# Two attention layers on one core: the second layer's attention in one piece, the first layer's steps between projections, position pieces further apart

## The chip, the core and the metric

The kernel runs on one core of one Trainium2 chip. The metric is device time in microseconds (us), as the median of several runs; lower is better. Everything is fp32 (one operand pair is fp32r), and eight images go through two attention layers.

## What is computed

Two residual layers, each `x + attention(group_norm(x))`, over 8 images of 32 x 32 positions and 512 channels. The first layer has 16 heads of 32 channels and a projection; the second has 4 heads of 128 channels and adds logits of relative position, one for rows and one for columns. Cut from the reference:

```python
def _L0_conv_ref(x, w_qkv, w_proj, b_proj):
    qkv = xt @ w_qkv                                 # q, k, v: 16 heads of 32
    attn = jax.nn.softmax(jnp.einsum('bhid,bhjd->bhij', q * SCALE, k), axis=-1)
    out = jnp.einsum('bhij,bhjd->bhid', attn, v)
    return out @ w_proj + b_proj
def _L1_conv_ref(x, Wq, Wk, Wv, Wo, pos_emb_w, pos_emb_h):
    q = x @ Wq * scale; k = x @ Wk; v = x @ Wv       # 4 heads of 128
    scores = attn_q @ k + relative_logits(pos_q, pos_emb_w, pos_emb_h)
    return (jax.nn.softmax(scores, axis=-1) @ v) @ Wo
x = x + _L0_conv_ref(_gn(x), ...)
x = x + _L1_conv_ref(_gn(x), ...)
```

`_gn` is a group norm with 32 groups. Scores of one head are 1024 x 1024.

## The kernel before

An image is held channel-major (four tiles of 128 channels x 1024 positions). Its work is cut into stages, each a Python generator that records some instructions and then yields a number, the cost of what it recorded, in units of one group of four matmuls with 32 output columns:

- `load`: reads the image, transposes it on VectorE (DVE), takes statistics, norms it.
- `before_0`: q, k and v of the first layer, three matrix products. A product has 8 parts (`project_T`, `project_rows`); each part is 16 matmuls with 32 columns (`by_columns`, L206), one copy out of PSUM on ScalarE (ACT, L128), and a yield of 4.
- `attention_0`: 64 steps. A step is `front`, four matmuls of 32 rows into a four-bank tile `ps` (L278) and an exp of 128 x 2048 on ACT (L286), and then `back` of the step before: four matmuls of 32 columns into `acc` (L297) and an add to the running sum `es` on DVE (L306 the first time, L308 after). After every eight steps `finish` sums over partitions with four more matmuls (`su`, L317), takes a reciprocal and a check on DVE (L264, L245), and multiplies on GpSimd (L266).
- `after_0`, `norm_1`: the first layer's projection, added to the image on DVE (L482), and the second norm.
- `second`: q, k and v of the second layer. `position_logits` makes the position terms from q in four pieces. A piece is 64 small matmuls into a bank `pp` (L351, L358), then eight pairs of a cast on ACT (L373, into `posT`) and a subtraction on DVE (L374), both of which read `pp`. In the kernel before the pieces stand among the eight parts of the k product, after the second, fourth, sixth and eighth (`woven(keys, ..., 1, 2)`), and the v product follows.
- `attention_1`: 64 steps with full 128 x 128 matmuls: q times k (L387) and the position term (L388) into one bank, an exp of 128 x 512 on ACT (L390), e times v into `acc` (L399), a running sum on DVE (L408, L410), and every eight steps `su` (L418) with the same reciprocal, check and multiply.
- `after_1`: the second projection, added on DVE (L514), transposed (L516) and written out.

In what follows R stands for the four matmuls of L278, C for the four of L297, P for a part of a product, u for `su` of the first layer, x for the matmuls of a position piece, and F for the full-array matmuls of `attention_1`.

The stages of three images are recorded together. In round b, `side_by_side` walks through `attention_0` of image b and between its steps records from a chain of the other stages: `after_0`, `norm_1` and `second` of image b-1, with `after_1` of image b-2, then `attention_1` of image b-1 with the `load` of image b+1 woven into it, then `before_0` of image b+1. The total cost of that chain, divided by 65, is what is recorded after each attention step: rest is taken until `done` has caught up. In rounds 2 to 6 that is 408 units, 6.3 per step, of which `attention_1` is 144. A stage that yields 0 is taken whole at once, since nothing is counted as done. Rounds 0 and 8 have no partner on one side: in round 8, `attention_1` of the last image runs alone.

Tiles come from pools: three PSUM banks with the tag `bank` serve `pa`, `pp`, `su` and all of `attention_1`'s `ps` and `acc`; `ps` of the first layer is a single four-bank tile, so each R waits for the exp of the step before; `e0` has two buffers, so an exp waits for the add that last read the buffer it writes. The framework that records the instructions may move one ahead of others on its engine[...].

Of the kernel before, what the change touches and what calls it, by code (L numbers as in the profile page):

```python
# [9 lines left out]
F32 = mybir.dt.float32  # L10
# [7 lines left out]
P = 128  # L18
# [10 lines left out]
def quick_path(  # L29
# [100 lines left out]
    def load_weight(w, col0, name):  # L130
        t = mem.tile([P, CC, NB], F32, tag="w", name=name, bufs=2)
        nc.sync.dma_start(t, w.rearrange("(cc p) n -> p cc n", p=P)[:, :, col0 : col0 + NB])
        return t
# [76 lines left out]
    def project_T(xn, w, dsts, name):  # L210

        for m in range(CC):
            for h in range(NH):
                pa = bank(f"pa_{name}_{m}_{h}")
                for cc in range(CC):
                    by_columns(
                        pa,
                        w[:, cc, m * P : (m + 1) * P],
                        xn[cc][:, h * NB : (h + 1) * NB],
                        start=(cc == 0),  # L220
                        stop=(cc == CC - 1),
                    )
                evacuate(dsts(m)[:, h * NB : (h + 1) * NB], pa)
                yield CC

    def project_rows(xn, w, y, name):

        for t in range(NT):
            pa = bank(f"pa_{name}_{t}")
            for cc in range(CC):  # L230
                by_columns(
                    pa,
                    xn[cc][:, t * P : (t + 1) * P],
                    w[:, cc, :],
                    start=(cc == 0),
                    stop=(cc == CC - 1),
                )
            evacuate(y[:, t, :], pa)
            yield CC
# [100 lines left out]
    def position_logits(q, posT, b):  # L340

        qv = q.rearrange("p (i e) (x y) -> p e i x y", e=2, y=IW)
        G = NB // (IW * H1 // 2)
        for t in range(IW // G):
            pp = bank(f"pp_{b}_{t}", [P, G, H1 // 2, 32])
            for g in range(G):
                s = t * G + g
                for e in range(2):  # L350
                    nc.tensor.matmul(  # L351
                        pp[64 * e : 64 * e + 32, g],
                        pw_sb[:, IW - 1 - s : 2 * IW - 1 - s],
                        qv[:, e, :, :, s],
                        start=True,
                        stop=True,
                    )
                    nc.tensor.matmul(  # L358
                        pp[64 * e + 32 : 64 * e + 64, g],
                        ph_sb[:, IH - 1 - s : 2 * IH - 1 - s],  # L360
                        qv[:, e, :, s, :],
                        start=True,
                        stop=True,
                    )
            for h in range(H1):
                e, i = h % 2, h // 2
                by_y = posT[h].rearrange("p (x y) -> p y x", y=IW)
                by_x = posT[h].rearrange("p (x y) -> p x y", y=IW)
                for u, view in enumerate((by_y, by_x)):
                    view = view[:, t * G : (t + 1) * G]  # L370
                    rows = slice(64 * e + 32 * u, 64 * e + 32 * u + 32)
                    rests = slice(64 * (1 - e) + 32 * u, 64 * (1 - e) + 32 * u + 32)
                    nc.scalar.copy(view[rows], pp[rows, :, i])  # L373
                    nc.vector.tensor_sub(view[rests], pp[rows, :, i], view[rows].bitcast(F32))  # L374
            yield 2

    def attention_1(q, k, v, posT, b):

        steps = [(h, c, j) for h in range(H1) for c in range(NH) for j in range(NT)]
        state = {}  # L380

        def front(h, c, j):
            name = f"1_{b}_{h}_{c}_{j}"
            ps = bank(f"ps_{name}")
            keys = slice(j * P, (j + 1) * P)
            queries = slice(c * NB, (c + 1) * NB)
            nc.tensor.matmul(ps, k[h][:, keys], q[:, h, queries], start=True, stop=False)  # L387
            nc.tensor.matmul(ps, sel[:, keys], posT[h][:, queries], start=False, stop=True)  # L388
            e = mem.tile([P, NB], F32, tag="e1", name=f"e_{name}", bufs=3)
            nc.scalar.activation(e, ps, AF.Exp, scale=1.0 / math.sqrt(D1))  # L390
            return e

        def back(h, c, j, e):
            name = f"1_{b}_{h}_{c}_{j}"
            if j == 0:
                state["acc"] = bank(f"acc_{name}")
                state["first"] = e
            acc = state["acc"]
            nc.tensor.matmul(  # L399
                acc,  # L400
                v[:, j, h * D1 : (h + 1) * D1],
                e,
                start=(j == 0),
                stop=(j == NT - 1),
            )
            if j == 1:
                state["esum"] = mem.tile([P, NB], F32, tag="es1", name=f"es_{name}", bufs=2)
                nc.vector.tensor_add(state["esum"], state["first"], e)  # L408
            elif j > 1:
                nc.vector.tensor_add(state["esum"], state["esum"], e)  # L410
            if j < NT - 1:
                return
            state["ended"] = (h, c, hold(acc, name), state["esum"])

        def finish(h, c, held, esum):
            name = f"1_{b}_{h}_{c}"
            su = bank(f"su_{name}")
            nc.tensor.matmul(su, ones, esum, start=True, stop=True)  # L418
            normalise(q[:, h, c * NB : (c + 1) * NB], held, su, name)

        pending = None
        for at in steps:
            e = front(*at)
            ended = state.pop("ended", None)
            if pending is not None:
                back(*pending)
            pending = (*at, e)
            if ended is not None:
                finish(*ended)
            yield 2.25  # L430
        back(*pending)
        yield 1
        finish(*state.pop("ended"))

    def load(b, st):
# [56 lines left out]
    def second(b, st):  # L492

        xn = st.pop("xn")
        q = st["ao"] = mem.tile([P, H1, N], F32, tag="block", name=f"q1_{b}", bufs=BLOCKS)
        yield from project_T(xn, load_weight(Wq, 0, f"wq1_{b}"), lambda m: q[:, m, :], f"q1_{b}")
        posT = [chunk(f"posT_{b}_{h}", dtype=F32R) for h in range(H1)]
        k = [chunk(f"k1_{b}_{m}") for m in range(CC)]
        keys = project_T(xn, load_weight(Wk, 0, f"wk1_{b}"), k.__getitem__, f"k1_{b}")
        yield from woven(keys, position_logits(q, posT, b), 1, 2)  # L500
        v = mem.tile([P, NT, C], F32, tag="block", name=f"v1_{b}", bufs=BLOCKS)
        yield from project_rows(xn, load_weight(Wv, 0, f"wv1_{b}"), v, f"v1_{b}")
        st["at"] = (q, k, v, posT, b)

    def after_1(b, st):

# [18 lines left out]
    def woven(main, side, start, gap):  # L525

        for at, cost in enumerate(main):
            if at >= start and (at - start) % gap == 0:
                cost += next(side, 0)
            yield cost  # L530
        yield from side
# [27 lines left out]


    PRODUCT = 8 * CC
    SECOND = 3 * PRODUCT + 8 + 2.25 * H1 * NH * NT

    states = [{} for _ in range(B)]
    run(load(0, states[0]))
# [1 line left out]
    for b in range(B + 1):  # L567
        rest, total = [], 0
        s = [None] * 2 + states + [None] * 2
        past, last, here, coming = s[b : b + 4]  # L570
        incoming = load(b + 1, coming) if coming is not None else iter(())
        if last is not None:
            rest.append(after_0(b - 1, last))
            norm = norm_1(b - 1, last)
            if past is not None:
                rest.append(woven(after_1(b - 2, past), norm, 1, 1))
                total += PRODUCT
            else:
                rest.append(woven(iter(()), norm, 0, 1))
            rest.append(second(b - 1, last))  # L580
            rest.append(woven(later(lambda st: attention_1(*st.pop("at")), last), incoming, 4, 6))
            total += PRODUCT + SECOND
        else:
            rest.append(incoming)
        if coming is not None:
            rest.append(before_0(b + 1, coming))
            total += 3 * PRODUCT
        if here is not None:
            side_by_side(attention_0(here["q"], here["k"], here["v"], b), chain(*rest), total)
        else:  # L590
            run(chain(*rest))
# [493 lines left out]
```

## Time and profile before

| | |
|---|---|
| median of 3 runs | 4242.93 us (4241.28 to 4242.94) |
| the profiled execution | 4241.89 us |
| its span, first to last instruction | 4239.9 us |
| mean granted TensorE clock | 0.993 |
| busy: DVE, ACT, GpSimd | 2314.6, 1673.7, 248.7 us |
| L278 R, L297 C, 4096 matmuls each | 610.1, 553.3 us busy |
| L286 exp of the first layer, 512 | 1879 ns each |
| L308 running sum of the first layer, 384 | 2316 ns each |
| L264 reciprocal, 128 | 3355 ns each |
| L373 cast, L374 subtraction of the position pieces, 256 each | 480, 511 ns each |

Busy times are unions of an engine's intervals. The end of a matmul is modelled, so the distance from the start of one group to the start of the next is the better measure of what TensorE (PE) spends on it, and that is what is used below. A stage can be cut out by its times: in round 3, for instance, the k and v products with the position pieces last from about 1502 to 1596 us, the second layer's attention from 1596 to 1791 us, and the products for the next image from there to 1906 us. The last image's attention, alone, is at 4065 to 4198 us.

### The profile page before, as it was taken

To read this page: it belongs to the slowest core of one execution; us is meant where nothing else is said; L and a number is where in the kernel's file an instruction comes from. 1 tells how busy PE (TensorE), PEld (TensorE's weight loads), DVE (VectorE), ACT (ScalarE), POOL (GpSimd) and SP (SyncE) were. 2 spreads that over 40 slices of the span, in tenths; PEclk is the share of its full clock that TensorE was granted. 3 is DMA by queue.
4 is the path that set the end of the run, shared out by engine and by line. 5 is a ranking of instruction groups with operands and counts; after the bars stand their busy time and mean duration, and the time that the engine had idled before them with its cause. 6 is when DMAs were issued, how large, how long until landed. Compare 5 with 4: busy or idle time off the path is not lost.

```text
span 4239.9 us, 66880 instructions
## 1 busy us (share of the span) xinstructions
PE 4111.0 (97%) x29890; PEld 1367.7 (32%) x29890; DVE 2314.6 (55%) x2105; ACT 1673.7 (39%) x1793; POOL 248.7 (6%) x155
## 2 busy tenths in 40 slices
PE   7999999999999999999999999999999999999998
PEld 2222333223332233322333223332233322333343
DVE  2566566354763547635576355663556635467334
ACT  1553444324443244432444324443344333444131
POOL 0000000000000000100000000000000000000000
PEclk9999999999999999999999999999999999999999
DMA  4101110131101311012110121102210022000301
GB/s 120 36 21 46 31 40 1 36 95 31 40 1 41 90 31 40 1 56 75 37 34 1 72 61 44 26 1 75 65 51 1 1 81 65 22 35 1 86 16 21
DMA packets 320904, 172.23 MB, mean 41 GB/s; under 512 B 271424, under 2 KB 271456, under 8 KB 320608
## 3 DMA queue, kind: packets, MB, share of 16 engines
q1 hardware_dynamic: 320512, 167.81, 13.9%
q8 instruction: 236, 3.87, 0.4%
q14 instruction: 60, 0.49, 0.0%
q0 software_dynamic: 96, 0.07, 0.0%
HBM read 117.51 MB, written 50.33 MB: 40 GB/s over the span
## 4 chain that ended last, share of the span: by engine, by line
PE 85%; DVE 8%; ACT 4%; issue 1%; DMA 0%; POOL 0%; SPq 0%; DVEq 0%; ACTq 0%; POOLq 0%
PE ps L278 11%; PE pa_q L206 10%; PE ps L387 10%; PE pp L206 10%; PE acc L297 10%; PE acc L399 10%; PE pa_v L206 10%; PE pa_k L206 7%; ACT e L286 3%; PE ps L388 3%; DVE rc L264 2%; DVE posT L374 2%; DVE es L308 2%; ACT posT L373 2%; PE su L317 1%
## 5 line engine op out<-in xcount | busy, mean ns | idle before, releaser
L308 DVE TENSOR_TENSOR es<-es,e 128x2048 f32<-128x2048 f32 x384 | 889.2, 2316 | 893.8 <-ACT e L286 893.5
L286 ACT ACTIVATE e<-ps 128x2048 f32<-128x2048 f32 x512 | 962.1, 1879 | 818.1 <-PE ps L278 702.4
L278 PE MATMUL ps<-q,k 32*128 32x512 f32 x4096 | 610.1, 645 | 58.4 <-ACT e L286 58.2
L264 DVE RECIPROCAL rc<-su 128x512 f32<-128x512 f32 x128 | 429.2, 3355 | 306.1 <-PE su L317 287.3
L387 PE MATMUL ps<-q,k 128*128 128x512 f32 x1024 | 548.3, 617 | 14.2 <-DVE checks L245 13.6
L297 PE MATMUL acc<-e,v 128*32 128x512 f32 x4096 | 553.3, 611 | 1.0 <-ACT e L286 1.0
L390 ACT ACTIVATE e<-ps 128x512 f32<-128x512 f32 x512 | 305.3, 598 | 563.9 <-PE ps L388 460.4
L399 PE MATMUL acc<-e,v 128*128 128x512 f32 x1024 | 525.7, 596 | 0.7 <-ACT e L390 0.7
L266 POOL TENSOR_TENSOR q<-hd,rc 128x512 f32<-128x512 f32 x128 | 226.6, 1770 | 3467.1 <-DVE rc L264 3265.2
L388 PE MATMUL ps<-posT,sel 128*128 128x512 f32 x512 | 406.9, 795 | 0.0
L410 DVE TENSOR_TENSOR es<-es,e 128x512 f32<-128x512 f32 x384 | 277.0, 721 | 163.2 <-ACT e L390 152.5
L278 PEld LDWEIGHTS ps<-q,k 32*128 32x128 f32 x4096 | 166.1, 183 | 455.0 <-issue 202.3
L387 PEld LDWEIGHTS ps<-q,k 128*128 128x128 f32 x1024 | 174.3, 189 | 339.7 <-issue 261.5
L128 ACT COPY q<-pa_q 128x512 f32<-128x512 f32 x128 | 75.0, 586 | 427.2 <-PE pa_q L206 427.2
L206 PE MATMUL pa_q<-x0T,wq 128*32 128x512 f32 x2048 | 237.0, 600 | 5.4 <-DMA wq<-in_L_conv_w_qkv 4.7
L399 PEld LDWEIGHTS acc<-e,v 128*128 128x128 f32 x1024 | 193.0, 190 | 151.2 <-issue 110.4
L374 DVE TENSOR_TENSOR posT<-pp,posT 32x256 fp32r<-32x256 f32 x256 | 130.9, 511 | 195.0 <-ACT posT L373 193.1
L206 PE MATMUL pa_v<-wv,x1T 128*32 128x512 f32 x2048 | 230.5, 598 | 2.9 <-DVE posT L374 2.9
L206 PE MATMUL pa_k<-x1T,wk 128*32 128x512 f32 x2048 | 231.9, 595 | 0.6
L206 PE MATMUL pa_k<-x0T,wk 128*32 128x512 f32 x2048 | 232.3, 592 | 0.0
L206 PE MATMUL pa_v<-wv,x0T 128*32 128x512 f32 x2048 | 231.6, 592 | 0.0
L206 PE MATMUL pa_q<-x1T,wq 128*32 128x512 f32 x2048 | 228.3, 595 | 3.1 <-DVE x1T L192 3.1
(67 smaller groups left out, 2614.9 us busy)
## 6 DMA issues: line engine op xcount, KB each, us to landing
xs<-in_x SPq DMA_DIRECT2D x128, 128.0 KB, 3.2
d<-x0T SPq DMA_DIRECT2D x32, 512.0 KB, 3.6
x1T<-d SPq DMA_DIRECT2D x32, 512.0 KB, 5.9
d<-x1T SPq DMA_DIRECT2D x32, 512.0 KB, 2.6
x2T<-d SPq DMA_DIRECT2D x32, 512.0 KB, 6.3
out<-ot SPq DMA_DIRECT2D x256, 64.0 KB, 1.9
wq<-in_L_conv_w_qkv SPq DMA_DIRECT2D x8, 1024.0 KB, 7.7
wk<-in_L_conv_w_qkv SPq DMA_DIRECT2D x8, 1024.0 KB, 5.8
```

What stands on the lines that cost most here:

```text
L206: nc.tensor.matmul(out[columns, :], weights[:, columns], moving, start=start, stop=stop)
L264: nc.vector.reciprocal(rec, su)
L266: nc.gpsimd.tensor_tensor(dst, held, rec, op=ALU.mult)
L278: nc.tensor.matmul(ps[:, r, :], k[m][rows, j * P : (j + 1) * P], q[m][rows, h * NB : (h + 1) * NB], start=True, stop=True,)
L286: nc.scalar.activation(e, ps, AF.Exp, scale=D0 ** -0.5)
L297: nc.tensor.matmul(acc[r * D0 : (r + 1) * D0, :], v[:, j, c0 : c0 + D0], e[:, r, :], start=(j == 0), stop=(j == NT - 1),)
L308: nc.vector.tensor_add(state["esum"], state["esum"], e)
L387: nc.tensor.matmul(ps, k[h][:, keys], q[:, h, queries], start=True, stop=False)
L388: nc.tensor.matmul(ps, sel[:, keys], posT[h][:, queries], start=False, stop=True)
L390: nc.scalar.activation(e, ps, AF.Exp, scale=1.0 / math.sqrt(D1))
L399: nc.tensor.matmul(acc, v[:, j, h * D1 : (h + 1) * D1], e, start=(j == 0), stop=(j == NT - 1),)
L410: nc.vector.tensor_add(state["esum"], state["esum"], e)
```

## The change

Every step of `attention_1` now yields 0, so the whole of it is recorded between two steps of `attention_0`; `SECOND` loses its share, and the remaining rest, 264 units in rounds 2 to 6, is spread over the same 65 slots, 4.1 per step. The position pieces are woven into the k and v products together, after parts 2, 6, 10 and 14 of 16 instead of 2, 4, 6 and 8 of 8. In round 1, where the second norm has no other stage beside it, each of its two yields counts 12 units.

```diff
@@ attention_1
             if ended is not None:
                 finish(*ended)
-            yield 2.25
+            yield 0
         back(*pending)
-        yield 1
+        yield 0
         finish(*state.pop("ended"))
@@ second
         k = [chunk(f"k1_{b}_{m}") for m in range(CC)]
-        keys = project_T(xn, load_weight(Wk, 0, f"wk1_{b}"), k.__getitem__, f"k1_{b}")
-        yield from woven(keys, position_logits(q, posT, b), 1, 2)
-        v = mem.tile([P, NT, C], F32, tag="block", name=f"v1_{b}", bufs=BLOCKS)
-        yield from project_rows(xn, load_weight(Wv, 0, f"wv1_{b}"), v, f"v1_{b}")
-        st["at"] = (q, k, v, posT, b)
+        st["at"] = at = [q, k, None, posT, b]
+
+        def keys_and_values():
+            yield from project_T(xn, load_weight(Wk, 0, f"wk1_{b}"), k.__getitem__, f"k1_{b}")
+            at[2] = mem.tile([P, NT, C], F32, tag="block", name=f"v1_{b}", bufs=BLOCKS)
+            yield from project_rows(xn, load_weight(Wv, 0, f"wv1_{b}"), at[2], f"v1_{b}")
+
+        yield from woven(keys_and_values(), position_logits(q, posT, b), 1, 4)
@@ rounds
     PRODUCT = 8 * CC
-    SECOND = 3 * PRODUCT + 8 + 2.25 * H1 * NH * NT
+    SECOND = 3 * PRODUCT + 8
+
+    ALONE = 12
...
             else:
-                rest.append(woven(iter(()), norm, 0, 1))
+                rest.append(cost + ALONE for cost in norm)
+                total += 2 * ALONE
```

## The prediction, made before the changed kernel ran

> **What bounds the kernel now.** I read the page first, then the stages by windows, then the order of starts on PE, then ACT's and DVE's timelines at the position pieces.
>
> ```profile
> PE 4111.0 (97%) x29890; PEld 1367.7 (32%) x29890; DVE 2314.6 (55%) x2105; ACT 1673.7 (39%) x1793; POOL 248.7 (6%) x155
> PE 85%; DVE 8%; ACT 4%; issue 1%; DMA 0%; POOL 0%; SPq 0%; DVEq 0%; ACTq 0%; POOLq 0%
> ...
> 1502.00:1596.00 94.00, 88.28 (x961) 30.08 (x954) 50.44 (x53) 45.69 (x62) 6.45 (x2) 1.00 0.12 34
> 1596.00:1791.00 195.00, 191.51 (x740) 73.75 (x742) 133.59 (x127) 87.43 (x99) 15.04 (x11) 1.00 0.09 22
> ...
> 4066.00:4197.00 131.00, 131.00 (x332) 61.50 (x331) 68.12 (x77) 42.34 (x71) 10.70 (x7) 1.00 0.00 1
> ```
>
> PE is the bound; what can move is its idle time and what it loses between unlike groups. The windows are, in round 3, k and v with the position pieces, then the second layer's attention mixed with first-layer steps, and the last image's attention alone, where PE never stops. DMA is idle enough to leave aside.
>
> ```profile
> 1600.15 1.02 PE L399 MATMUL acc<-e,v 128*128 128x512 f32 x2
> 1601.01 1.02 PE L387 MATMUL ps<-q,k 128*128 128x512 f32 x2
> ...
> 1602.10 1.02 PE L399 MATMUL acc<-e,v 128*128 128x512 f32 x2
> ...
> 1604.04 1.02 PE L399 MATMUL acc<-e,v 128*128 128x512 f32 x2
> 1604.99 1.14 PE L278 MATMUL ps<-q,k 32*128 32x512 f32 x8
> 1606.07 1.07 PE L297 MATMUL acc<-e,v 128*32 128x512 f32 x8
> 1607.06 1.12 PE L387 MATMUL ps<-q,k 128*128 128x512 f32 x2
> ...
> 1608.26 1.02 PE L399 MATMUL acc<-e,v 128*128 128x512 f32 x2
> ...
> 1833.35 1.06 PE L297 MATMUL acc<-e,v 128*32 128x512 f32 x8
> 1834.23 3.62 PE L206 MATMUL pa_k<-x0T,wk 128*32 128x512 f32 x32
> 1837.78 1.14 PE L278 MATMUL ps<-q,k 32*128 32x512 f32 x8
> ```
>
> Read the starts. Within `attention_1` an L399 pair takes 0.86 ahead of L387 (1600.15 to 1601.01) and 0.95 ahead of R (1604.04 to 1604.99); L387 with L388 takes 1.09 after L399 (1601.01 to 1602.10) and 1.20 after C (1607.06 to 1608.26); C takes 0.99 ahead of L387 and 0.88 ahead of P; P takes 3.55 ahead of R and 3.43 ahead of its like. R takes 1.07. So the step costs 1.07 + 0.88 everywhere, plus 0.09 + 0.11 + 0.11 = 0.31 inside F and 0.11 inside P.
>
> ```profile
> 1510.52 1.14 PE L278 MATMUL ps<-q,k 32*128 32x512 f32 x8
> ...
> 1515.35 1.90 ACT L286 ACTIVATE e<-ps 128x2048 f32<-128x2048 f32 x1
> 1517.31 1.14 PE L278 MATMUL ps<-q,k 32*128 32x512 f32 x8 [1.22 <-ACT e L286]
> ...
> 1558.43 1.89 ACT L286 ACTIVATE e<-ps 128x2048 f32<-128x2048 f32 x1
> ...
> 1560.36 2.29 DVE L308 TENSOR_TENSOR es<-es,e 128x2048 f32<-128x2048 f32 x1 [1.12 <-ACT e L286]
> 1562.68 0.42 DVE L374 TENSOR_TENSOR posT<-pp,posT 32x256 fp32r<-32x256 f32 x1
> 1564.83 1.88 ACT L286 ACTIVATE e<-ps 128x2048 f32<-128x2048 f32 x1
> ...
> ACT posT L373 <- DVE posT L374: 20.3, 22, 2.5
> ```
>
> This is the wait that decides the case. A piece's casts and subtractions alternate: a cast, its subtraction, the next cast, some 2.1 us for two pairs. The exp of the R behind the piece stands after the fifth cast and ends 6.75 us after R's start; the next R starts at 6.79. And the second exp ends 6.4 us after the first (1560.32 to 1566.71), because the sixth subtraction stands behind the running sum that needs the first exp, and the seventh cast waits for it.
>
> [...] in an open stretch an exp starts 1.20 us after its R (1832.28 to 1833.48); the one above started 4.83 us after it, behind casts. [...]
>
> **The change, part by part.** The built program's queues show that it does what it says: in rounds 1 to 7 the 64 steps of `attention_1` stand in one run, with only one R split over it.
>
> *1. Mode changes.* Before, some 165 of the 512 first-layer steps stand inside F (143 R directly after an L399 pair, 20 after L418); after, 7. Each saves 0.31 - 0.11 = 0.20: 160 x 0.20 = 32; with other small shifts of order, -31.
>
> *2. `attention_1`.* In round 3: 64 steps x (1.09 + 0.86) = 124.8, 8 L418 pairs at 0.86 = 6.9, 23.5 R and C with their changes at 2.26 = 53.1, three u at 0.9 = 2.7, sum 187.5; it took 195. So 7.5 of stalls and split groups per round (5.6 to 7.8 in rounds 1 to 6, 3.3 in round 7, drops of the clock taken off: 47 in all). Alone it lost 1.4. After, each of rounds 1 to 6 has this 1.4, and an R split as 1, 2 and 1 matmuls, where one alone takes a whole slot (1.05 instead of 0.27): 2.1, and 0.3 for the norm's two small matmuls. 6 x 3.8 + 1.4 = 24, so -23, and -3 for the half R that stands at the start of the next stage now. The `load` moves with it: its transposes and statistics stay ahead of the run on DVE, its DMAs on SP keep their order against the weights, and nothing on PE needs them for 100 us, so they cost nothing; were that cover gone, four transposes and statistics are about 11 us per round. DVE is busy 68 of 131 us in such a run, by the last window, and GpSimd's multiply (1770 ns) comes every 16 us.
>
> *3. Position pieces, and denser steps around them.* This is the loss. The steps are now nearer to each other (4.1 units of rest instead of 6.3): between two R there is C and one P, 1.07 + 0.88 + 3.55 = 5.50 us, as at 1832.28 to 1837.78. Each piece holds up two exps, so two R wait, and as C and P stand behind R on PE, the whole wait counts. From the order of the queues in rounds 2 to 6, with R after the piece at 0:
> - piece 1: R, C, u, a quarter group of P, and already the next R: 1.07 + 0.88 + 0.86 + 0.33 = 3.14, against 6.78: 3.64. Behind that the second exp overwrites the first buffer of the running sum; the add that frees it stands behind the casts, a reciprocal (3.36) and its check (0.77), and ends at 13.3; exp to 15.2, R ready at 13.2: 2.0.
> - piece 2: room 5.50: 1.28. A transpose (1.24) stands in the chain: second exp to 13.7, room 6.78 + 5.50 = 12.28: 1.45.
> - piece 3: the reciprocal of a u just before delays the first subtraction; exp after four casts, to 6.24: 0.79; second to 13.7 against 11.79: 1.96.
> - piece 4: room 1.07 + 0.88 + 1.07 + 0.11 = 3.14 again: 3.64; second exp 6.4 later, 13.1 against 6.78 + 1.95 + 2.47 = 11.2: 1.9.
>
> Sum 16.7 (adding the eight). Now the same stage loses 6.5 in these rounds (1.3 + 0.3 + 0.4 + 0.4 + 0.8 + 3.3, from the starts): +10.2, five times, +51. Round 1: 8.0 now; by the same count 2.6 + 5.5 + 5.7 + 2.1 = 15.9, +8. Round 7 has 168 units of rest, so R every 4.3 us: 8.1 + 6.0 + 5.5 + 5.5 = 25, now 10.7, +14.5. Round 8: the last piece ends two P (6.9) before L388 needs it, +1.4. Together +75. The second waits are the uncertain ones: without them 26 remain.
>
> *4. ALONE.* Only round 1; the scheduler fills the gaps with P. A stall of 4 us there may go or double: 0.
>
> Sum: -31 - 26 + 75 = +18. On the profiled execution's 4241.89 that is 4260; it stands 1 us under the median of the runs, so 4260 serves for both. The rest of the kernel (first-layer q, k, v, both projections) stays without stalls: at 5.5 us per step ACT has 1.88 + 0.59, DVE at most 2.3 + 0.75 + 0.8 + 0.5 = 4.4.
>
> **Rivals.**
> - *Only the first exp after a piece is late* (the second R finds room). For it: in round 3 now, second waits are short, 0.3 and 0.4. Against: there the next R stood further off. Its place is the sixth subtraction: it decides if DVE comes to that one early enough for the second exp to end within 5.5 us of the first. -31 - 26 + 26 = -31: 4211, so not slower.
> - *The losses just cancel.* The pieces cost two thirds of my count: +57 instead of +75 gives 4242. For it: DVE may do an add earlier than I have it.
> - *Faster still:* each piece stalls PE only as it does now: -57, 4185. Against: the 3.14 us rooms.
> - *Slower by far:* the denser steps make ACT and DVE late outside the pieces too. If each of 24 steps per round between the projections and q waited 0.5 us, 6 rounds x 12 = +72 on top: 4332. [...] I count 4.4 of 5.5, so it is unlikely.
>
> **How the numbers follow.** A measurement of this kernel can tell some 0.2%, 8.5 us, from no change. My forecast, 4252 to 4278, 0.55; cancel (4234 to 4251), 0.17; first exp only, 0.14; faster still, 0.04; slower by far, 0.10. The range, 4215 to 4285, takes in the first two, and from the others the nearer parts, some 0.08; 0.2 is left out. Faster 0.18, same 0.17, slower 0.65. The likeliest case's own range is 4252 to 4278.
>
> **What would show it.** A window over one round's `attention_1`: about 135 us with PE busy throughout; between pieces, R to R at 5.50. L278's idle on the exp, 58.2 us on the page, should rise to some 130; that is the line to look at. If it stays near 58, part 3 is wrong and the time is about 4190; if L388 or L206 shows waits on `posT` instead, the bank, not the exp, is what I missed.

## The result and the profile after

| | before | after |
|---|---|---|
| median of 6 runs | 4242.63 us (4240.91 to 4243.90) | 4274.40 us (4271.40 to 4277.93) |
| ratio to before | | 1.0077 [1.0064, 1.0089] |
| span of the profiled execution | 4239.9 us | 4269.6 us |
| mean granted TensorE clock in it | 0.993 | 0.991 |

The change makes the kernel 0.8% slower. The forecast was 4260 us, with a range of 4215 to 4285.

From the page of after, the busy times, the shares of the chain of waits, and the groups of R and L387 (busy time, mean ns of one, idle time before them and what ended most of it):

```profile
PE 4110.6 (96%) x29890; PEld 1391.3 (33%) x29890; DVE 2322.2 (54%) x2105; ACT 1676.7 (39%) x1793; POOL 257.4 (6%) x155
...
PE 85%; DVE 8%; ACT 5%; issue 1%; DMA 0%; POOL 0%; SPq 0%; DVEq 0%; ACTq 0%; POOLq 0%
...
L278 PE MATMUL ps<-q,k 32*128 32x512 f32 x4096 | 610.3, 650 | 101.3 <-ACT e L286 101.0
...
L387 PE MATMUL ps<-q,k 128*128 128x512 f32 x1024 | 535.1, 604 | 6.3 <-ACT e L390 5.7
```

The same two groups on the page of before:

```profile
L278 PE MATMUL ps<-q,k 32*128 32x512 f32 x4096 | 610.1, 645 | 58.4 <-ACT e L286 58.2
...
L387 PE MATMUL ps<-q,k 128*128 128x512 f32 x1024 | 548.3, 617 | 14.2 <-DVE checks L245 13.6
```

PE is busy as long as before (4111.0), though the blocks it works through are cheaper now, and it idles longer. Two lines moved: R now waits 101.0 us for the exp instead of 58.2, and L387 no longer waits for the check of a sum, which before was 13.6 us of its 14.2 us of idle time.

Windows over after, in round 3 the k and v stage and the run of `attention_1`, and then `attention_1` of the last image (the columns are the window, its length, the busy times, PEclk, the DMA share and GB/s):

```profile
1524.00:1647.00 123.00, 110.39 (x1085) 35.00 (x1078) 68.84 (x69) 60.26 (x70) 4.42 (x2) 0.96 0.16 45
1647.00:1784.00 137.00, 136.03 (x350) 63.27 (x354) 78.28 (x90) 42.94 (x73) 12.96 (x9) 1.00 0.07 15
4094.00:4228.00 134.00, 133.43 (x340) 62.17 (x343) 69.19 (x80) 43.91 (x75) 10.66 (x7) 1.00 0.00 0
```

PEclk is the granted clock of TensorE as a share of full speed. The middle line is the gain: 137 us at full clock, PE idle for 1.0 of them, and as good as alone (third line). The first line is the loss: 12.6 us of idle time in 123, at a mean clock of 0.96.

The starts on PE can be accounted for completely. Call each R, C, P and so on a block. Give each block the start-to-start duration that it has in stretches without idle time (the durations of the prediction), sum them over the order of each kernel, and divide what is left between PE's idle time, the half clock (what blocks took longer that a drop of the granted clock to 0.50 touched), and the rest, which is mostly matmul groups that were split:

| us | before | after | difference |
|---|---|---|---|
| sum of the blocks | 4034.3 | 4003.1 | -31.2 |
| idle | 89.8 | 120.2 | +30.4 |
| split groups and small rests | 50.3 | 69.0 | +18.7 |
| half clock | 25.9 | 37.4 | +11.5 |
| sum | | | +29.4 (spans: +29.7) |

By stage, the excess over the blocks (idle time, half clock and rest together) went from 63.5 to 136.5 in k and v with the pieces, from 57.3 to 24.4 in `attention_1`, and by +12.8 in the projections and q of round 7.

The wait at a piece, read from the timelines of PE, ACT and DVE of after at the first piece of round 4:

```profile
2060.52 1.14 PE L278 MATMUL ps<-q,k 32*128 32x512 f32 x8
...
2063.34 1.02 PE L206 MATMUL pa_k<-x1T,wk 128*32 128x512 f32 x2
...
2064.88 0.58 ACT L373 CAST posT<-pp 32x256 fp32r<-32x256 f32 x1 [0.49 <-DVE posT L374]
2065.27 1.89 ACT L286 ACTIVATE e<-ps 128x2048 f32<-128x2048 f32 x1
...
2066.11 3.36 DVE L264 RECIPROCAL rc<-su 128x512 f32<-128x512 f32 x1
...
2067.21 1.14 PE L278 MATMUL ps<-q,k 32*128 32x512 f32 x8 [2.86 <-ACT e L286]
...
2071.30 2.29 DVE L306 TENSOR_TENSOR es<-e,e 128x2048 f32<-128x2048 f32 x1
...
2073.71 1.88 ACT L286 ACTIVATE e<-ps 128x2048 f32<-128x2048 f32 x1 [2.04 <-DVE es L306]
...
2075.64 1.56 PE L278 MATMUL ps<-q,k 32*128 32x512 f32 x8 [2.00 <-ACT e L286]
```

R is done at 2061.6, but its exp starts behind the fifth cast, 4.75 us after R's start, where the exp of the R before it started 1.21 us after its own (2053.02 to 2054.23); the next R starts at 2067.21, 6.69 us after the first. The second exp waits for the running sum, which stands behind the reciprocal and two more subtractions, so a second R is late. Its matmuls take 1.56 instead of 1.14: the clock drops to 0.50 while they run, at 2076.27 (shown in the last section).

### The profile page after: what moved, and what is told of

It is laid out like the page before. It is cut to its first block, busy times and chain, and to the rows that moved or that the text cites. A ratio compares the mean times of both kernels' runs of the same rounds, so it can differ in the third digit from the quotient of the medians.

```text
span 4269.6 us, 67060 instructions
## 1 busy us (share of the span) xinstructions
PE 4110.6 (96%) x29890; PEld 1391.3 (33%) x29890; DVE 2322.2 (54%) x2105; ACT 1676.7 (39%) x1793; POOL 257.4 (6%) x155
## 4 chain that ended last, share of the span: by engine, by line
PE 85%; DVE 8%; ACT 5%; issue 1%; DMA 0%; POOL 0%; SPq 0%; DVEq 0%; ACTq 0%; POOLq 0%
PE ps L278 11%; PE pa_q L206 10%; PE ps L387 10%; PE pp L206 10%; PE acc L399 10%; PE acc L297 10%; PE pa_k L206 9%; PE pa_v L206 8%; ACT e L286 3%; PE ps L388 3%; DVE rc L264 3%; DVE posT L374 2%; ACT posT L373 2%; DVE es L308 1%; PE su L317 1%; DVE es L306 1%
## 5 line engine op out<-in xcount | busy, mean ns | idle before, releaser
L308 DVE TENSOR_TENSOR es<-es,e 128x2048 f32<-128x2048 f32 x384 | 879.7, 2291 | 748.0 <-ACT e L286 748.0
L278 PE MATMUL ps<-q,k 32*128 32x512 f32 x4096 | 610.3, 650 | 101.3 <-ACT e L286 101.0
L387 PE MATMUL ps<-q,k 128*128 128x512 f32 x1024 | 535.1, 604 | 6.3 <-ACT e L390 5.7
L266 POOL TENSOR_TENSOR q<-hd,rc 128x512 f32<-128x512 f32 x128 | 237.1, 1853 | 3734.6 <-DVE rc L264 3490.6
L410 DVE TENSOR_TENSOR es<-es,e 128x512 f32<-128x512 f32 x384 | 285.8, 744 | 267.1 <-ACT e L390 265.5
L278 PEld LDWEIGHTS ps<-q,k 32*128 32x128 f32 x4096 | 165.7, 185 | 518.7 <-issue 285.2
L387 PEld LDWEIGHTS ps<-q,k 128*128 128x128 f32 x1024 | 183.8, 189 | 270.8 <-issue 183.9
L206 PE MATMUL pa_k<-x1T,wk 128*32 128x512 f32 x2048 | 245.6, 598 | 1.0 <-ACT k L128 0.9
L206 PE MATMUL pa_v<-wv,x1T 128*32 128x512 f32 x2048 | 245.4, 596 | 0.0
L206 PE MATMUL pa_q<-x1T,wq 128*32 128x512 f32 x2048 | 237.7, 593 | 4.4 <-DVE x1T L192 4.4
L206 PE MATMUL pp<-q,wo 128*32 128x512 f32 x2048 | 234.5, 592 | 2.9 <-DVE checks L245 2.9
```

Of the source, the lines that this page charges most:

```text
L206: nc.tensor.matmul(out[columns, :], weights[:, columns], moving, start=start, stop=stop)
L266: nc.gpsimd.tensor_tensor(dst, held, rec, op=ALU.mult)
L278: nc.tensor.matmul(ps[:, r, :], k[m][rows, j * P : (j + 1) * P], q[m][rows, h * NB : (h + 1) * NB], start=True, stop=True,)
```

## Experiments

Each ratio is to runs of the kernel before on the same chip.

| run | median us | ratio, 95% |
|---|---|---|
| e1 one piece only | 4272.25 | 1.0076 [1.0059, 1.0093] |
| e2 gap only | 4246.25 | 1.0010 [1.0003, 1.0017] |
| e3 casts on DVE | 4213.50 | 0.9936 [0.9919, 0.9952] |
| e4 before, casts on DVE | 4189.95 | 0.9880 [0.9863, 0.9896] |
| e6 no ALONE | 4280.10 | 1.0092 [1.0076, 1.0109] |
| e7 last round mixed | 4258.20 | 1.0036 [1.0022, 1.0050] |
| e8 DVE casts, later pieces | 4220.82 | 0.9955 [0.9938, 0.9972] |
| e9 e8 and e7 | 4198.69 | 0.9901 [0.9885, 0.9918] |
| e10 a product part behind each piece | 4213.85 | 0.9934 [0.9921, 0.9948] |
| e11 that, DVE casts, last round mixed | 4169.55 | 0.9829 [0.9816, 0.9843] |

### Which part of the change costs: e1 and e2

e1 is the kernel after with the pieces back in the k product:

```diff
-        yield from woven(keys_and_values(), position_logits(q, posT, b), 1, 4)
+        keys = project_T(xn, load_weight(Wk, 0, f"wk1_{b}"), k.__getitem__, f"k1_{b}")
+        yield from woven(keys, position_logits(q, posT, b), 1, 2)
+        at[2] = mem.tile([P, NT, C], F32, tag="block", name=f"v1_{b}", bufs=BLOCKS)
+        yield from project_rows(xn, load_weight(Wv, 0, f"wv1_{b}"), at[2], f"v1_{b}")
```

> The kernel after, with its position pieces where they were before (gap 2, in the k product alone); attention_1 still gives no steps away, ALONE stays. Theory (it is the denser first-layer steps that make the exps late, not where the pieces stand): by the order of its queues round 3 has 3.64 + 2.0 at piece 1, 1.28 + 0.4 at piece 2, 3.64 + some 1.5 at piece 3, 0.4 + 2.0 at piece 4, about 14.5 per round against the 16.2 measured after; so 4255 to 4275 us, close to the kernel after. Rival A (pieces spaced further apart are the loss): the k and v stage falls back to the 63 us of stalls it had before, so about 4201. Rival B (attention_1 in one piece is itself the loss, wherever the pieces are): 4274 as well, so this run tells A from the two others.

e2 is the kernel before with only that part of the change (its `yield 2.25`, `SECOND` and the missing `ALONE` stay):

```diff
-        yield from woven(keys, position_logits(q, posT, b), 1, 2)
-        yield from project_rows(xn, load_weight(Wv, 0, f"wv1_{b}"), v, f"v1_{b}")
+        yield from woven(keys_and_values(), position_logits(q, posT, b), 1, 4)
```

> The kernel before, with only the position pieces further apart (gap 4, over k and v); attention_1 gives steps away as before. Theory: the steps keep their old spacing, so an R behind a piece mostly has 5.50 us of room or more; stalls per round 5 to 7 as before: 4235 to 4250. Rival A (the spacing of the pieces is the loss): 4242 + 73 = 4315. Rival B (attention_1 in one piece is the loss): 4242.

Undoing the gap leaves e1 at after's ratio (1.0076 against 1.0077). Doing it alone costs 4.9 us. So the spacing of the pieces is neither the loss nor a remedy. The loss comes with the steps that left `attention_1`. The L278 groups on the pages of e1 and of e2 say the same:

```profile
L278 PE MATMUL ps<-q,k 32*128 32x512 f32 x4096 | 609.8, 650 | 102.7 <-ACT e L286 102.5
```

```profile
L278 PE MATMUL ps<-q,k 32*128 32x512 f32 x4096 | 609.3, 645 | 74.6 <-ACT e L286 74.4
```

e1 waits for the exp as long as after does. e2 waits 16 us longer than before on this line; its span, 4248.2, is 8.3 us longer, with a mean clock of 0.994 instead of 0.993.

### What the exp waits behind: e3 and e4

One line of the kernel after (e3) and of the kernel before (e4):

```diff
-                    nc.scalar.copy(view[rows], pp[rows, :, i])
+                    nc.vector.tensor_copy(view[rows], pp[rows, :, i])
```

> The kernel after, with the casts of the position pieces (L373) on VectorE, next to their subtractions, so no exp stands behind a cast on ScalarE and a pair needs no hand-over. Theory: the waits of L278 on the exp at the pieces go (most of the 136 us of the k and v stages and of the drops of the clock behind them); VectorE takes 16 operations of about 0.42 us per piece, some 7 us, and the running sums behind them are late by that but have two buffers; 4150 to 4185 us, L278's idle on the exp under 30 us. Rival B (denser steps make ScalarE and VectorE late everywhere): VectorE has 107 us more, the waits stay or move to the running sum: 4265 or more.

> The kernel before, with the same casts on VectorE. Theory: its 63 us of stalls in the k and v stages mostly go, 4185 to 4205, and the kernel after with the same edit is the faster of the two by 20 to 50 us, since fewer mode changes and the unmixed attention_1 remain as its gain. Rival B: the kernel after with this edit stays slower than this one by some 30 us.

The wait on the exp went, as expected: on e3's page

```profile
L278 PE MATMUL ps<-q,k 32*128 32x512 f32 x4096 | 601.1, 641 | 25.5 <-ACT e L286 25.4
...
L206 PE MATMUL pa_k<-x1T,wk 128*32 128x512 f32 x2048 | 256.1, 604 | 16.0 <-DVE checks L245 15.7
```

L278's idle time falls from 101.0 to 25.4. This shows the theory's core: R waited on ACT, because the exp stood behind the casts there. The time fell by 61 us, though, not by 89 or more, and e4, which came out where it was expected, stayed faster than e3 by 23.5 us. So the expectation that the change is a gain once the casts are off ACT was wrong. The second line has the reason: a new wait, on a bank. The timelines of DVE and PE in e3 at the first piece of round 4:

```profile
2040.94 0.61 DVE L373 CAST posT<-pp 32x256 fp32r<-32x256 f32 x1
2041.58 3.36 DVE L264 RECIPROCAL rc<-su 128x512 f32<-128x512 f32 x1
...
2046.03 0.69 DVE L245 CUSTOM_DVE_ANT_0 jk<-su,rc 128x512 f32<-128x512 f32 x1
...
2046.87 3.48 PE L206 MATMUL pa_k<-x1T,wk 128*32 128x512 f32 x10 [3.15 <-DVE checks L245]
```

The reciprocal of a u right behind the piece stands behind thirteen of the piece's sixteen casts and subtractions on DVE. P needs u's bank and waits 3.15 us for the check. With the drop of the clock behind it (3.48 us for ten records of P that take 1.88 in after at 3494.61) and a late R (1.18 us), this one place costs 7.0 us per round; the other three pieces cost 0.8 together. The pairs of cast and subtraction run no faster on one engine: two take 2.12 us here (2035.79 to 2037.91), and 2.11 us on two engines in after (2060.67 to 2062.78). The gain is only that the exp stands elsewhere.

### Other places: e8 and e9

e8 is e3 with `woven(..., 2, 4)`, so that no u stands behind a piece in rounds 1 to 6. e9 has e7's edit (below) as well.

> The kernel after with the casts on VectorE as in e3, and with the pieces one slot of the product later (start 2 instead of 1), so that in rounds 1 to 6 no u stands right behind a piece. Theory: what e3 kept was a bank held by u, whose reciprocal stands behind the casts and subtractions on VectorE (L206 waits 3.15 us for the check, an R 1.18 us more, with a drop of the clock: 7.0 us per round); with u elsewhere six rounds lose that no more, round 7 keeps its loss or has some more: 4165 to 4185. Rival (VectorE is simply too full behind a piece, whatever stands there): the wait moves to the exp or to another part: 4205 or more.

> e8 with the last round mixed as in e7. Theory: its gains add up, e8's time less 20 to 30 us: 4140 to 4162, the fastest of all so far, with the 31 us of mode changes (less 6) and attention_1 unmixed standing as gains against the kernel before with casts on VectorE, 4190. Rival: they don't add, since round 7's waits are VectorE's then: 4165 or more.

e8's rival was right: 4220.82, no better than e3. The k and v stages lost 3.7 us in rounds 2 to 6 instead of some 8.7, but `attention_1` lost 7.0 to 8.7 instead of 4.5. In e8's timelines of DVE and PE, at the start of `attention_1` in round 4:

```profile
2132.63 1.25 DVE L443 STREAM_TRANSPOSE x0T<-xs 128x1024 f32<-128x1024 f32 x1
...
2134.39 1.13 PE L387 MATMUL ps<-q,k 128*128 128x512 f32 x2 [0.98 <-DVE posT L374]
...
2138.39 3.36 DVE L264 RECIPROCAL rc<-su 128x512 f32<-128x512 f32 x1
...
2143.05 1.10 PE L387 MATMUL ps<-q,k 128*128 128x512 f32 x2 [3.32 <-DVE checks L245]
```

The last piece now stands one slot before the end. There it meets the transposes and statistics of the `load` and another u, and the same reciprocal holds the same kind of bank a little later. e9 came out 22.1 us below e8: e7's gain adds to it as expected, on a base that was some 45 us off.

### The room behind a piece: e10 and e11

e10 leaves the casts on ACT and changes the pacing alone. A piece counts less than it costs, so the next step comes one P later:

```diff
                     nc.vector.tensor_sub(view[rests], pp[rows, :, i], view[rows].bitcast(F32))
-            yield 2
+            yield -4
...
-    SECOND = 3 * PRODUCT + 8
+    SECOND = 3 * PRODUCT - 16
```

> The kernel after, casts on ScalarE as there, with only the pacing changed: each position piece counts -4 units instead of 2 (SECOND less 24), so that a product part stands behind every piece before the next first-layer step, and the steps elsewhere are a little denser (some 3.7 units apart instead of 4.1). Theory (the loss is the missing room behind a piece): the casts run to some 8.4 us after the piece, R starts at 3.55, its exp ends at some 10.4, the next R has room to 9.05, so each piece costs some 1.3 to 1.7 us, 6 per round against the 16 to 18 now; round 7 is no better; model sum +4: 4205 to 4235. Rival D (8.4 us of casts on ScalarE block the exps wherever the steps stand, so the wait moves to the next R): 4260 or more.

Timelines of PE and ACT in e10 at the first piece of round 4:

```profile
2043.58 3.63 PE L206 MATMUL pa_k<-x1T,wk 128*32 128x512 f32 x30
...
2047.14 1.14 PE L278 MATMUL ps<-q,k 32*128 32x512 f32 x8
...
2051.53 0.36 ACT L373 CAST posT<-pp 32x256 fp32r<-32x256 f32 x1
2051.92 1.88 ACT L286 ACTIVATE e<-ps 128x2048 f32<-128x2048 f32 x1
...
2053.85 1.14 PE L278 MATMUL ps<-q,k 32*128 32x512 f32 x8 [1.13 <-ACT e L286]
```

The piece ends at 2043.3, P fills the time to 2047.14, the exp starts behind the eighth cast, and the next R waits 1.13 us. There is no second late R. Each of the round's four pieces loses 1.4 to 1.6 us, where 1.3 to 1.7 was expected, 6.0 in all against 16.2 in after. At the start of the stage some 2 us more go at no piece: the denser pacing puts an R only 3.8 us behind the one before it, and the next R waits 1.26 us for its exp. With the same casts on the same engine the whole kernel is 60.6 us faster than after, by the pacing alone, and 0.7% faster than the kernel before. Rival D is out.

e11 is e10 with e3's line and e7's edit:

> The same pacing, with the casts on VectorE and with the last round mixed as in e7. Theory: no exp stands behind casts, no u and no R right behind a piece, so the running sums and reciprocals behind VectorE's 16 operations find room, apart from the piece that meets the load's transposes; the k and v stages lose 0 to 3 us per round, round 7 as in e9: 4145 to 4178, faster than both kernels and than e4 (4190). Rival (VectorE is too full in these stages, as in e8): the waits stand at other places, 4185 to 4205.

4169.55 us, inside the theory's interval, and the fastest version here: 1.7% faster than the kernel before, and below e4 (0.9829 against 0.9880, intervals apart). Windows of e11 over round 4, the k and v stage and then `attention_1`:

```profile
2018.00:2111.00 93.00, 91.74 (x985) 34.39 (x984) 73.41 (x91) 33.52 (x30) 6.27 (x2) 1.00 0.16 44
2111.00:2251.00 140.00, 138.59 (x370) 63.60 (x372) 81.24 (x97) 45.36 (x74) 11.43 (x8) 1.00 0.09 21
```

PE idles 1.3 us in the stage in which it idled 12.6 us of after's round 3, though DVE is busy 73 of 93 us there.

### Round 7 and ALONE: e7 and e6

e7, the kernel after:

```diff
-            yield 0
+            yield 2.25 if b == B - 2 else 0
...
             total += PRODUCT + SECOND
+            if b == B - 1:
+                total += 2.25 * H1 * NH * NT
```

> The kernel after, but in its last round with first-layer steps (round 7, which has no next image to project) attention_1 gives steps away as in the kernel before, 2.25 units each. Theory (density is the cause): round 7 gets back before's spacing; 32.5 - 15.8 of stalls in its k and v stage and the 12.9 us outside the pieces go, attention_1 loses 1.8 more, mode changes come back at 6.1 us: 4252, between 4245 and 4260. Rival (the dense steps cost nothing outside the pieces, the 12.9 us are another thing): 4262 to 4274.

4258.2, 16.2 us below after; the 12.9 us outside the pieces of round 7 are gone to 0.1. They had been taken for waits, but for the most part they are not. In after's timeline of PE, in `after_0` of round 7:

```profile
3494.61 1.88 PE L206 MATMUL pp<-q,wp 128*32 128x512 f32 x10
3496.42 1.14 PE L278 MATMUL ps<-q,k 32*128 32x512 f32 x8
...
3498.38 2.76 PE L206 MATMUL pp<-q,wp 128*32 128x512 f32 x22
3501.07 1.14 PE L278 MATMUL ps<-q,k 32*128 32x512 f32 x8
```

R stands inside a part P, after 5 of its 16 matmuls (a matmul is two records). In after's trace the records of four matmuls of P start within 0.02 us of each other, and the next four records 0.43 us later. The one matmul ahead of R has its two records 0.43 us apart all the same, and so have the three behind R. So a group of four cut into 1 and 3 takes the time of two groups here: 1.81 + 2.69 = 4.50 instead of 3.55 (0.11 of the difference is that P stands ahead of an R twice instead of once). The timeline shows no idle time in it. There are 12 such cuts in the projections and q of round 7, together 10.3 us, and two waits of R on the exp, together 2.6 us.

e6 is the kernel after with `ALONE = 0`:

> The kernel after with ALONE at 0: in round 1 the two slots in which the norm stands alone give no extra first-layer steps. Theory: ALONE is worth nothing (0 within 4 us, the prediction's step 4): round 1's after_0 and q lose 5.8 us again instead of 8.9, the rest stands: 4268 to 4276. Rival C (ALONE costs what the kernel after lost): 4262 or less; if ALONE hides a real gap, 4280 or more.

4280.10, 5.7 us above after: outside the range of the theory, and just past the bound from which ALONE was to hide a real gap. The intervals (1.0076 to 1.0109, and 1.0064 to 1.0089) overlap, so it isn't shown that ALONE gains anything. It certainly doesn't cost what after lost. Round 1 lost 2.6 us more without it, and the rest of the difference in the two profiles lies in the k and v stages of the later rounds, where the half clock took 27 us instead of 21 over rounds 2 to 6.

## Why the prediction was right, and what it missed

1. *Mode changes, -31.* A mode change is here what a group takes more, start to start, ahead of one unlike it: 0.09 to 0.11 us in the starts of before. The sum of the blocks over the new order is -31.2, and 0.20 us for each of some 160 moved steps comes within 1 us of it. As the blocks have the prediction's own durations, this checks the count of moved steps; the price of a change rests on the starts read there, and no run took it apart or showed where it comes from.
2. *`attention_1`, -23, and -3 behind it.* The stage lost 24.4, as worked out (24). It gained 32.9 rather than 23, because 10.3 us of half clock that stood there before, and that the prediction had taken off, went too. The stage behind it lost 2.0 more instead of 3 less.
3. *Pieces, +75.* Measured +73.0. In round 4 the waits, start to start less the blocks, were 3.55 + 2.07, 1.22 + 1.47, 0.47 + 2.01 and 3.53 + 1.89, sum 16.2, where 3.64 + 2.0, 1.28 + 1.45, 0.79 + 1.96 and 3.64 + 1.9 were predicted. e3 and e10 show that the cause is the predicted one: the exp behind the casts, and the room behind the piece. That the sum hits is in part luck, because its parts differ: this term had neither drops of the clock nor split groups in it. Of the 73, 41 are idle time, 21 the half clock and 11 split groups, 7 of these in round 7. Where a drop of the clock followed the first wait, the second was shorter or gone, since the matmuls between took longer: at the first piece of round 5 in after, R waited 2.87 us, a drop began 1.0 us after its start, and the next R waited 0.34 us; in round 4 the two waited 2.86 and 2.00 us, with no drop between. The two R start 8.41 and 8.43 us apart. The totals of equal rounds differ by 3.4 us at most. As neither slow matmuls nor split groups show as idle time, L278's idle time rose to 101.0 and not to some 130.
4. *ALONE, 0.* Round 1 in front of k and v lost 3.1 more; within the 4 us that were allowed.

So the four terms of the sum hold: they came to some +14 instead of +18, and nearly all the rest of the +29.4 is what the sum had put at nothing. The step that failed is the sentence behind the sum, that the rest of the kernel "stays without stalls: at 5.5 us per step". In round 7 a step comes every 2.6 units of rest, less than a part of a product (4), and so falls inside one. That cost 12.8 us there, and in `after_1` of the other rounds a small group and a short wait cost some 4 more in all. The prediction had priced exactly this split for an R in `attention_1` (1.05 instead of 0.27; in before one matmul of R alone takes 1.05, 2253.28 to 2254.33), but not for P. With it, 4260 would have been 4273 to 4277.

Of the rivals, "the losses just cancel" (its +57 is three quarters of the count of 75, not two thirds) and "faster still" fall by the time, "only the first exp is late" by the second waits above, and "slower by far" by the idle time outside the pieces, which stayed small: in the projections and q of round 7 the exp was late twice, 2.6 us in all, and the cut parts cost the other 10.3 us.

What stays open: how much of the 20 us between e4 and e11 is due to the mode changes alone, since e11 also has the pieces' new pacing, and no run gives that pacing to the kernel before.

## What to carry to other kernels

Packing work of one kind together removed its mixing cost here (31.2 us in the sum of the blocks), but what it was mixed with got denser elsewhere: count the room between two steps where a long chain on another engine meets them, wait by wait, before moving anything. A helper chain that alternated between two engines delayed what was queued behind it on both: at the first piece of round 4 the exp on ACT started 4.75 us after its R instead of 1.21, and the running sum on DVE 4.14 us after that exp's end (2067.16 to 2071.30), where the next one started 0.03 us after its own (2075.59 to 2075.62). Give such a chain a stretch in which nothing behind it is urgent (e10), before moving it to another engine (e3), which here moved a part of the wait to that engine's queue. When a filler is cut to let a step in, the border between two groups of four matmuls is the place that the cuts of round 7 suggest (4.50 us where a group was cut, 3.55 whole); no run here tried it.

## What the runs showed of the hardware

- *2 us of idle time within one window of 3.413 us were followed by a drop of the clock, and where the idle time fell decided.* In after, each of the 18 drops before the end of the work is 3.413 us long or twice that, and the starts of all of them lie on one grid of 3.413 us, to 0.01 us. Windows of after on this grid, in round 4:

```profile
2062.62:2066.03 3.41, 1.74 (x14) 0.22 (x2) 1.69 (x4) 2.10 (x4) 0.00 (x0) 1.00 0.00 0
2066.03:2069.44 3.41, 2.23 (x20) 0.73 (x24) 3.38 (x2) 1.50 (x2) 0.00 (x0) 1.00 0.00 0
2069.44:2072.86 3.42, 3.42 (x36) 1.04 (x32) 3.29 (x6) 0.98 (x2) 1.28 (x1) 1.00 0.00 0
2072.86:2076.27 3.41, 1.41 (x16) 0.31 (x8) 1.81 (x3) 2.35 (x2) 0.00 (x0) 1.00 0.00 0
2076.27:2079.68 3.41, 3.41 (x21) 0.60 (x17) 2.11 (x2) 1.88 (x1) 0.00 (x0) 0.50 0.00 0
```

  The wait of 2.86 us that ends at 2067.21 lies across a border, 1.67 us of idle time on one side and 1.18 on the other, and no drop follows. The wait of 2.00 us that ends at 2075.64 lies whole in the fourth window, and the fifth is at 0.50 for 3.41 us while PE is busy throughout. Cut in this way from 420 us on, after has 12 windows at full clock with more than 2.00 us of idle time, and a drop follows each of them; of the five with 1.80 to 2.00 a drop follows four, of the 1088 with less none. In the profiles of all twelve kernels together the counts are 87 of 87, 22 of 33 and 8 of 13076. The eight, with 1.1 to 1.3 us of idle time, are all in the kernel before and in e4 (one drop is that at 2255.0 before), and in each of these windows one matmul of a split R runs alone; whether such a matmul counts for less than a full group, no run tested. e10's waits of R at the pieces in rounds 2 to 6, 1.03 to 1.22 us each, were followed by no drop.
- *A wait therefore cost different amounts in equal rounds.* Rounds 2 to 6 run the same program, yet their k and v stages lost 18.1, 19.7, 17.9, 16.3 and 16.4 us in after's profile, 1.9 to 5.5 us of it at half clock, as the same waits lie differently on the grid. In e10, whose shorter waits were followed by no drop there, the five stages lost the same within 0.1 us. Its runs lie within 2.6 us of each other, after's within 6.5.
